# Two graph layers on one core: W1 moved behind the attention sum, softmax rows transposed through VectorE and DRAM

## The chip, the core and the metric

The kernel runs on one NeuronCore of a Trainium2 chip. The metric is the time of one launch in device microseconds, the median of several runs. The profile is that of one execution, whose span is counted from the first to the last instruction. The engines are TensorE (PE in the profile, its weight loads PEld), VectorE (DVE), ScalarE (ACT), GpSimd (POOL) and SyncE (SP, which only issues DMAs here). [...]

## What is computed

There are 16 batches of 1024 nodes with 512 features, one dense 1024 x 1024 matrix adj with about 6% nonzeros, and two layers. All is float32. The reference, cut to what matters:

```
# layer 0
h = relu(layernorm(x));  x = x + (adj @ h) @ weight + bias
# layer 1
h = relu(layernorm(x)) @ W
s1, s2 = h @ a1, h @ a2                       # a1, a2: the halves of a
e = leaky_relu(s1[:, :, None] + s2[:, None, :], 0.2) * adj
h_prime = softmax(e, axis=2) @ h
x = x + elu(h_prime + beta * h)
```

## The kernel before

The nodes of a batch are 8 chunks of 128 rows, two halves of 4 chunks. For each batch the kernel does this:

- norm0_part and norm0_end (lines 143 to 155) make hn, the normalised input of layer 0, with nodes on the partitions. GpSimd adds the bias to x in place (line 148).
- y_half (line 157) multiplies hn with the transposed adj (adjT, made once by transpose_adj on TensorE at the start): 4 x 8 products for a half of the nodes. The result yT has features on the partitions.
- out0 (line 173) multiplies yT with W0 for one chunk, adds x, and takes the statistics of the new x.
- h_transposes (line 191) makes u, the normalised input of layer 1 without its 1/std, transposes it on TensorE through an identity (group ut) and copies it to uT. h_products (line 201) multiplies uT with W1 to hw, and forms the row sums s1 and s2 against a1 and a2. diag (line 221) is s2 on the diagonal of a 128 x 128 tile.
- spread_s2 (line 230) multiplies ones with diag, which gives s2 of all nodes on each partition (group pb).
- softmax_row (line 242) makes one chunk of exp(e - max) and 1/sum. adj lies in SBUF all the time (adj_sb).
- row_transposes (line 260) transposes that chunk on TensorE in 8 pieces (group pt); ScalarE copies them to pT.
- attend (line 269) multiplies pT with hw, adds beta times hw, applies elu and adds x; the result is stored from SP.

The loop over batches (line 309) puts layer 0 of batch b+1 beside layer 1 of batch b. The order on each engine isn't only that of the source: the builder of the program orders the instructions of each engine when they have become ready, with the source's order as priority, and adds all waits. A tile of a pool waits for a free buffer among the pool's.

A float32 product of 128 x 128 with 128 x 512 is two MATMUL instructions in the profile; a transpose is one.

Of the kernel before, what the change touches and what calls it, by code (L numbers as in the profile page):

```python
"""Two pre-norm graph layers: x + (adj @ relu(LN(x))) W0 + bias, then x + elu(GAT(relu(LN(x)))).

All matrix products are float32 on the tensor engine.  The nodes (1024) are cut into 8 chunks of
128; chunk c of a batch holds nodes c*128 .. c*128+127 on the partitions.

Layer 0 of batch b+1 is interleaved with layer 1 of batch b, so that the tensor engine has matrix
products while the other engines work on norms and softmax rows.
"""
# [10 lines left out]
F32 = mybir.dt.float32  # L19
# [3 lines left out]
P = 128  # L23
ALPHA = 0.2
EPS = 1e-5
# [4 lines left out]
def kernel(  # L30
# [13 lines left out]
    NCH = N // P  # chunks of nodes  # L44
    DC = D // P  # chunks of features
    HC = NCH // 2  # chunks of nodes in a half
    HN = N // 2

    const = ctx.enter_context(tc.tile_pool(name="const", bufs=1))
    xpool = ctx.enter_context(tc.tile_pool(name="xpool", bufs=5))  # L50
    big = ctx.enter_context(tc.tile_pool(name="big", bufs=1))
    work = ctx.enter_context(tc.tile_pool(name="work", bufs=2))
    stat = ctx.enter_context(tc.tile_pool(name="stat", bufs=2))
    ps_y = ctx.enter_context(tc.tile_pool(name="ps_y", bufs=2, space=bass.MemoryType.PSUM))
    ps_t = ctx.enter_context(tc.tile_pool(name="ps_t", bufs=3, space=bass.MemoryType.PSUM))
    ps_m = ctx.enter_context(tc.tile_pool(name="ps_m", bufs=3, space=bass.MemoryType.PSUM))

# [1 line left out]
    ident = const.tile([P, P], F32, name="ident")  # L59
    make_identity(nc, ident)  # L60
    ones = const.tile([P, P], F32, name="ones")
    nc.gpsimd.memset(ones, 1.0)
    eps_c = const.tile([P, 1], F32, name="eps_c")
    nc.gpsimd.memset(eps_c, EPS)
# [3 lines left out]
    def load_x(b, h, engine):  # L68
        t = xpool.tile([P, HC, D], F32, tag="x", name=f"x_{b}_{h}")
        engine.dma_start(  # L70
            out=t, in_=x[b, h * HN : (h + 1) * HN, :].rearrange("(c p) d -> p c d", p=P)
        )
        x_tiles[b, h] = t

    def xc(b, c):
        return x_tiles[b, c // HC][:, c % HC, :]

    adj_sb = [const.tile([P, N], F32, name=f"adj_{c}") for c in range(NCH)]
    adjT = [const.tile([P, N], F32, name=f"adjT_{c}") for c in range(NCH)]
    load_x(0, 0, nc.scalar)  # L80
    for c in range(HC):
        nc.sync.dma_start(out=adj_sb[c], in_=adj[ts(c, P), :])
    load_x(0, 1, nc.scalar)
    w0_sb = const.tile([P, DC, D], F32, name="w0_sb")
    nc.scalar.dma_start(out=w0_sb, in_=w0.rearrange("(c p) o -> p c o", p=P))
    bias_bc = const.tile([P, D], F32, name="bias_bc")
    nc.scalar.dma_start(out=bias_bc, in_=bias.partition_broadcast(P))
    for c in range(HC, NCH):
        nc.sync.dma_start(out=adj_sb[c], in_=adj[ts(c, P), :])
    w1_sb = const.tile([P, DC, D], F32, name="w1_sb")  # L90
    nc.scalar.dma_start(out=w1_sb, in_=w1.rearrange("(c p) o -> p c o", p=P))
    a1_bc = const.tile([P, D], F32, name="a1_bc")
    nc.scalar.dma_start(out=a1_bc, in_=a[0:D, :].rearrange("f o -> (f o)").partition_broadcast(P))
    a2_bc = const.tile([P, D], F32, name="a2_bc")
    nc.scalar.dma_start(
        out=a2_bc, in_=a[D : 2 * D, :].rearrange("f o -> (f o)").partition_broadcast(P)
    )
    beta_c = const.tile([P, 1], F32, name="beta_c")
    nc.scalar.dma_start(out=beta_c, in_=beta.partition_broadcast(P))
# [7 lines left out]
    def transpose_adj(h):  # L107
        for mc in range(NCH):
            pt = ps_t.tile([P, HC, P], F32, tag="tr", name=f"adjt_{h}_{mc}")
            for k in range(HC):  # L110
                nc.tensor.transpose(pt[:, k, :], adj_sb[h * HC + k][:, ts(mc, P)], ident)
            copy(mc, adjT[mc][:, ts(h, HN)], pt.rearrange("p k n -> p (k n)"))

# [1 line left out]
    mvs = {}  # L115
    rstds = {}

    def stats(layer, b, c):
        if c == 0:
            mvs[layer, b] = stat.tile([P, NCH, 2], F32, tag=f"mv{layer}", name=f"mv{layer}_{b}")  # L120
        st = stat.tile([P, 6], F32, tag="bn", name=f"bn{layer}_{b}_{c}")
        nc.vector.bn_stats(st, xc(b, c))  # L122
        nc.vector.bn_aggr(mvs[layer, b][:, c, :], st)

    def inv_std(layer, b):
        mv = mvs[layer, b]
        sd = stat.tile([P, NCH], F32, tag=f"sd{layer}", name=f"sd{layer}_{b}")
        nc.scalar.activation(sd, mv[:, :, 1], AF.Sqrt, bias=eps_c)
        r = stat.tile([P, NCH], F32, tag=f"rstd{layer}", name=f"rstd{layer}_{b}")
        nc.vector.reciprocal(r, sd)  # L130
        rstds[layer, b] = r

    def centred_relu(dst, layer, b, c):
        """relu(x - mean): relu(LN(x)) without its positive factor 1/std."""
        nc.vector.tensor_scalar(  # L135
            dst, xc(b, c), mvs[layer, b][:, c, 0:1], 0.0, op0=ALU.subtract, op1=ALU.max
        )

# [1 line left out]
    hns = {}  # L140
    yTs = {}

    def norm0_part(b, c):
        stats(0, b, c)
        hn = big.tile([P, D], F32, tag=f"hn{c}", name=f"hn_{b}_{c}")
        centred_relu(hn, 0, b, c)
        hns[b, c] = hn
        nc.gpsimd.tensor_tensor(xc(b, c), xc(b, c), bias_bc, op=ALU.add)  # L148

    def norm0_end(b):  # L150
        inv_std(0, b)
        for c in range(NCH):
            nc.scalar.activation(
                hns[b, c], hns[b, c], AF.Copy, scale=rstds[0, b][:, c : c + 1]
            )

    def y_half(b, h):
        """yT[d, n] = sum_m hn[m, d] adj[n, m] for half of the nodes n."""
        yT = big.tile([P, DC, HN], F32, tag="yT", name=f"yT_{b}_{h}")
        for dc in range(DC):  # L160
            py = ps_y.tile([P, HN], F32, tag="py", name=f"py_{b}_{h}_{dc}")
            for mc in range(NCH):
                nc.tensor.matmul(  # L163
                    py,
                    hns[b, mc][:, ts(dc, P)],
                    adjT[mc][:, ts(h, HN)],
                    start=(mc == 0),
                    stop=(mc == NCH - 1),
                )
            copy(dc, yT[:, dc, :], py)  # L170
        yTs[b, h] = yT

    def out0(b, c):
        """x1 = x + bias + y W0, in place of x, and its statistics."""
        h, k = divmod(c, HC)
        po = ps_m.tile([P, D], F32, tag="pm", name=f"po_{b}_{c}")
        for dc in range(DC):
            nc.tensor.matmul(  # L178
                po, yTs[b, h][:, dc, ts(k, P)], w0_sb[:, dc, :],
                start=(dc == 0), stop=(dc == DC - 1),  # L180
            )
        nc.vector.tensor_tensor(xc(b, c), po, xc(b, c), op=ALU.add)  # L182
        stats(1, b, c)

# [1 line left out]
    hws = {}  # L186
    s1s = {}
    s2bcs = {}
    diags = {}

    def h_transposes(b, c):
        u = work.tile([P, D], F32, tag="u", name=f"u_{b}_{c}")
        centred_relu(u, 1, b, c)
        pt = ps_t.tile([P, DC, P], F32, tag="tr", name=f"ut_{b}_{c}")
        for dc in range(DC):
            nc.tensor.transpose(pt[:, dc, :], u[:, ts(dc, P)], ident)  # L196
        uT = work.tile([P, DC, P], F32, tag="uT", name=f"uT_{b}_{c}")
        copy(c, uT, pt)
        return uT

    def h_products(b, c, uT):
        """h = relu(LN(x1)) W1 with its row sums against a1 and a2."""
        ph = ps_m.tile([P, D], F32, tag="pm", name=f"ph_{b}_{c}")
        for dc in range(DC):
            nc.tensor.matmul(  # L205
                ph, uT[:, dc, :], w1_sb[:, dc, :], start=(dc == 0), stop=(dc == DC - 1)
            )
        hw = big.tile([P, D], F32, tag=f"hw{c}", name=f"hw_{b}_{c}")
        nc.scalar.activation(hw, ph, AF.Copy, scale=rstds[1, b][:, c : c + 1])  # L209
        hws[b, c] = hw  # L210
        if c == 0:
            s1s[b] = stat.tile([P, NCH], F32, tag="s1", name=f"s1_{b}")
            diags[b] = work.tile([P, NCH, P], F32, tag="e", name=f"diag_{b}")
        s2 = stat.tile([P, 1], F32, tag="s2", name=f"s2_{b}_{c}")
# [8 lines left out]
    def h_layer(b):  # L223
        uT = h_transposes(b, 0)
        for c in range(NCH):
            after = h_transposes(b, c + 1) if c + 1 < NCH else None
            h_products(b, c, uT)
            uT = after
# [152 lines left out]
```

## Time and profile before

| | |
|---|---|
| time, median of 3 runs | 2896.78 us (2895.94 to 2896.81) |
| span of the profiled execution | 2893.5 us |
| granted TensorE clock | 0.998 of full |
| read from and written to HBM | 40.63 MB, 33.55 MB |
| mean DMA traffic | 26 GB/s |
| ACT_TABLE_LOAD | 32, of 1.283 us |

A line of a group in the profile has the source line, engine and operation, then the tile written and those read, the shapes and the count; behind the first bar the time in total and the mean of one in ns; behind the second the idle time of the engine ahead of the group, and what ended it. A line of the timeline has the start in us, the duration, and in brackets the idle time ahead of it.

### The profile page before, as it was taken

The page shows a single profiled execution, that of the slowest core. Times are in us where ns is not written, and L with a number is a line of the kernel's source. Part 1 is how long each engine was busy: PE and PEld are TensorE (multiplying, and loading weights), DVE is VectorE, ACT ScalarE, POOL GpSimd, SP SyncE. Part 2 cuts the span into 40 slices and gives each one's busy share as a digit, 9 for nine tenths or more (in the row PEclk, how much of TensorE's full clock was granted, in tenths as well). Part 3 has the DMA queues.
Part 4 walks back from the last instruction along what each step waited for, and adds up shares of the span by engine and source line. Part 5 has one row for each costly group of instructions (what it writes and reads, how often), then busy time and mean ns, then how long its engine had stood idle before and what let it go on. Part 6 is the DMA issues. An engine that isn't in the chain of part 4 may idle for free.

```text
span 2893.5 us, 21399 instructions
## 1 busy us (share of the span) xinstructions
PE 2852.3 (99%) x7808; PEld 1344.7 (46%) x7808; DVE 1336.0 (46%) x2616; ACT 803.9 (28%) x1240; POOL 547.3 (19%) x520
## 2 busy tenths in 40 slices
PE   7999999999999999999999999999999999999988
PEld 3444444444444444444444444444444444444444
DVE  2364353643536344363543536435364353644444
ACT  1132232322323223232222323223232232322323
POOL 1112022130211203112031120312112022130213
PEclk9999999999999999999999999999999999999999
DMA  4001000000000000001010000000001000000000
GB/s 171 0 5 36 18 30 29 8 33 19 30 29 12 33 15 33 26 23 36 1 36 22 29 30 4 33 22 30 29 8 33 18 29 29 8 33 4 19 11 29
DMA packets 38216, 75.54 MB, mean 26 GB/s; under 512 B 2913, under 2 KB 2913, under 8 KB 38113
## 3 DMA queue, kind: packets, MB, share of 16 engines
q1 hardware_dynamic: 35424, 69.22, 7.0%
q10 hardware_dynamic: 2688, 4.98, 0.5%
q8 instruction: 61, 1.00, 0.1%
q14 instruction: 43, 0.34, 0.0%
HBM read 40.63 MB, written 33.55 MB: 26 GB/s over the span
## 4 chain that ended last, share of the span: by engine, by line
PE 93%; DVE 4%; ACT 2%; DMA 1%; issue 0%; POOLq 0%; POOL 0%; ACTq 0%; DVEq 0%
PE pa L275 30%; PE py L163 30%; PE ph L205 15%; PE po L178 12%; PE pt L265 4%; PE ut L196 2%; DVE e L246 1%; DVE e L248 1%; ACT e L255 1%; DVE x L182 1%; DMA bias_bc<-in_L_gnn_bias_dram 1%; ACT e L245 1%; DVE bn L122 0%; DVE s2bc L103 0%; DVE u L135 0%
## 5 line engine op out<-in xcount | busy, mean ns | idle before, releaser
L275 PE MATMUL pa<-hw,pT 128*128 128x512 f32 x2048 | 902.5, 592 | 0.0
L163 PE MATMUL py<-adjT,hn 128*128 128x512 f32 x2048 | 892.6, 593 | 0.0
L163 PEld LDWEIGHTS py<-adjT,hn 128*128 128x128 f32 x2048 | 386.9, 190 | 474.5 <-issue 461.1
L275 PEld LDWEIGHTS pa<-hw,pT 128*128 128x128 f32 x2048 | 380.6, 190 | 436.4 <-issue 429.4
L205 PE MATMUL ph<-w_sb,uT 128*128 128x512 f32 x1024 | 458.1, 592 | 0.2 <-ACT uT L105 0.2
L178 PE MATMUL po<-w_sb,yT 128*128 128x512 f32 x1024 | 449.8, 592 | 0.3 <-DVE yT L103 0.3
L280 POOL TENSOR_SCALAR t<-z 128x512 f32<-128x512 f32 x128 | 78.7, 615 | 1228.3 <-DVE z L279 1179.9
L178 PEld LDWEIGHTS po<-w_sb,yT 128*128 128x128 f32 x1024 | 194.4, 190 | 245.0 <-issue 243.9
L205 PEld LDWEIGHTS ph<-w_sb,uT 128*128 128x128 f32 x1024 | 187.0, 190 | 199.0 <-issue 194.9
L103 DVE COPY yT<-py 128x512 f32<-128x512 f32 x64 | 44.3, 692 | 477.7 <-PE py L163 477.7
L148 POOL TENSOR_TENSOR x<-x,bias_bc 128x512 f32<-128x512 f32 x128 | 166.5, 1314 | 416.9 <-DVE hn L135 315.6
L255 ACT ACTIVATE e<-e,nmx 128x1024 f32<-128x1024 f32 x128 | 147.2, 1150 | 321.8 <-DVE nmx L253 321.3
L246 DVE SCALAR_TENSOR_TENSOR e<-e 128x1024 f32<-128x1024 f32 x128 | 196.5, 1546 | 71.1 <-ACT e L245 68.2
L272 POOL TENSOR_SCALAR t<-hw,beta_c 128x512 f32<-128x512 f32 x128 | 139.1, 1086 | 469.6 <-ACT hw L209 460.5
L217 DVE CUSTOM_DVE_ANT_0 prod<-hw,a_bc 128x512 f32<-128x512 f32 x256 | 185.2, 723 | 89.3 <-ACT hw L209 86.0
L284 POOL TENSOR_TENSOR z<-z,x 128x512 f32<-128x512 f32 x128 | 162.2, 1267 | 227.8 <-DVE z L283 227.8
L266 ACT COPY pT<-pt 128x512 f32<-128x512 f32 x256 | 136.4, 584 | 221.6 <-PE pt L265 221.5
L209 ACT ACTIVATE hw<-ph,rstd 128x512 f32<-128x512 f32 x128 | 88.0, 687 | 390.7 <-PE ph L205 390.7
L283 DVE SCALAR_TENSOR_TENSOR z<-t,z 128x512 f32<-128x512 f32 x128 | 88.7, 693 | 217.2 <-ACT t L281 217.2
L279 DVE SCALAR_TENSOR_TENSOR z<-pa,rs,t 128x512 f32<-128x512 f32 x128 | 96.1, 751 | 178.9 <-PE pa L275 177.2
L122 DVE BATCH_NORM_STATS2 bn<-x 128x6 f32<-128x512 f32 x256 | 170.6, 684 | 16.3 <-DMA x<-in_x_dram 12.9
L248 DVE CUSTOM_DVE_ANT_0 e<-e,adj 128x1024 f32<-128x1024 f32 x128 | 173.9, 1360 | 2.3
(41 smaller groups left out, 1408.1 us busy)
## 6 DMA issues: line engine op xcount, KB each, us to landing
out_dram<-z SPq DMA_DIRECT2D x128, 256.0 KB, 2.0
x<-in_x_dram SPq DMA_DIRECT2D x30, 1024.0 KB, 6.0
adj<-in_adj_dram SPq DMA_DIRECT2D x8, 512.0 KB, 9.1
x<-in_x_dram ACTq DMA_DIRECT2D x2, 1024.0 KB, 12.6
w_sb<-in_L_gnn_weight_dram ACTq DMA_DIRECT2D x1, 1024.0 KB, 22.1
w_sb<-in_L_gnn_W_dram ACTq DMA_DIRECT2D x1, 1024.0 KB, 11.2
a_bc<-in_L_gnn_a_dram ACTq DMA_DIRECT2D x2, 256.0 KB, 5.7
bias_bc<-in_L_gnn_bias_dram ACTq DMA_DIRECT2D x1, 256.0 KB, 19.7
```

What stands on the lines that cost most here:

```text
L122: nc.vector.bn_stats(st, xc(b, c))
L148: nc.gpsimd.tensor_tensor(xc(b, c), xc(b, c), bias_bc, op=ALU.add)
L163: nc.tensor.matmul(py, hns[b, mc][:, ts(dc, P)], adjT[mc][:, ts(h, HN)], start=(mc == 0), stop=(mc == NCH - 1),)
L178: nc.tensor.matmul(po, yTs[b, h][:, dc, ts(k, P)], w0_sb[:, dc, :], start=(dc == 0), stop=(dc == DC - 1),)
L205: nc.tensor.matmul(ph, uT[:, dc, :], w1_sb[:, dc, :], start=(dc == 0), stop=(dc == DC - 1))
L217: nc.vector.tensor_tensor_reduce(out=prod, in0=hw, in1=a_bc, scale=1.0, scalar=0.0, op0=ALU.mult, op1=ALU.add, accum_out=s,)
L246: nc.vector.scalar_tensor_tensor(e, e, ALPHA, e, op0=ALU.mult, op1=ALU.max)
L248: nc.vector.tensor_tensor_reduce(out=e, in0=e, in1=adj_sb[c], scale=1.0, scalar=LOWEST, op0=ALU.mult, op1=ALU.max, accum_out=mx,)
L255: nc.scalar.activation(e, e, AF.Exp, bias=nmx, accum_out=sm)
L272: nc.gpsimd.tensor_scalar(t, hws[b, c], beta_c, 1.0, op0=ALU.mult, op1=ALU.mult)
L275: nc.tensor.matmul(pa, pT[:, jc, :], hws[b, jc], start=(jc == 0), stop=(jc == NCH - 1))
L284: nc.gpsimd.tensor_tensor(z, z, xc(b, c), op=ALU.add)
```

## The change

Layer 1 is regrouped. Since the attention sum is linear, softmax(e) @ (u W1) is (softmax(e) @ u) W1. So:

- u (with its 1/std) stays with nodes on the partitions and is the stationary operand of attend; the product with W1 comes behind, in out1. No u is transposed.
- s1 and s2 are dot products of u with W1 a1 and W1 a2 (v1_bc, v2_bc, made once through DRAM). spread_s2 writes s2 to DRAM and reads it back to all partitions.
- beta h is added by beta times the row's sum on the diagonal of the unnormalised softmax row.
- The softmax row is transposed in 32 x 32 blocks on VectorE. Four DMAs (one for each group of 32 partitions) write the blocks to DRAM and one reads them back into pT. A half of pT is one tile, and attend works on a half, as y_half does.
- adj isn't kept in SBUF; each softmax row loads its chunk again (two buffers, tag "adj").
- The leaky relu is one Prelu on ScalarE. 1/std is a power on GpSimd, for two chunks at a time. elu is formed from Relu and Exp.
- x is loaded twice, once for the norm (load_x, 4 buffers) and once with the bias as residual (load_res, 10 buffers). The tile zT shares a pool of 3 buffers with yT.

The core of the diff, the new lines:

```diff
+    def load_x(b, c):
+        t = xs.tile([P, D], F32, tag="x", name=f"x_{b}_{c}")
+        nc.sync.dma_start(out=t, in_=x[b, ts(c, P), :])
...
+    def load_res(b, c):
+        t = x1p.tile([P, D], F32, tag="x1", name=f"x1_{b}_{c}")
+        nc.sync.dma_start(out=t, in_=x[b, ts(c, P), :])
+        nc.gpsimd.tensor_tensor(t, t, bias_bc, op=ALU.add)
...
+    def inv_std(r, nb, mv):
+        k = r.shape[1]
+        nc.gpsimd.tensor_scalar(r, mv[:, :, 1], EPS, 1.0, op0=ALU.add, op1=ALU.mult)
+        nc.gpsimd.tensor_tensor(r, r, half[:, 0:k], op=ALU.pow)
+        nc.vector.scalar_tensor_tensor(nb, mv[:, :, 0], -1.0, r, op0=ALU.mult, op1=ALU.mult)
...
+    def out0(b, g):
...
+        inv_std(r, nb, mv)
+        for k in range(2):
+            c = 2 * g + k
+            u = nat.tile([P, D], F32, tag=f"u{c}", name=f"u_{b}_{c}")
+            nc.scalar.activation(
+                u, x1s[b, c], AF.Relu, scale=r[:, k : k + 1], bias=nb[:, k : k + 1]
+            )
+            us[b, c] = u
+            for v, s in ((v2_bc, s2s[b]), (v1_bc, s1s[b])):
...
+                nc.vector.tensor_tensor_reduce(
+                    out=prod, in0=u, in1=v, scale=1.0, scalar=0.0,
+                    op0=ALU.mult, op1=ALU.add, accum_out=s[:, c : c + 1],
+                )
...
+    def spread_s2(b):
+        d = dram.tile([N], F32, tag="s2d", name=f"s2d_{b}")
+        nc.sync.dma_start(out=d.rearrange("(c p) -> p c", p=P), in_=s2s[b])
+        t = work.tile([P, N], F32, tag="s2bc", name=f"s2bc_{b}", bufs=1)
+        nc.sync.dma_start(out=t, in_=d[:].partition_broadcast(P))
...
+    def softmax_row(b, c):
...
+        w = work.tile([P, N], F32, tag="adj", name=f"adj_{b}_{c}")
+        nc.sync.dma_start(out=w, in_=adj[ts(c, P), :])
+        e = work.tile([P, N], F32, tag="e", name=f"e_{b}_{c}", bufs=3)
+        nc.scalar.activation(e, s2bcs[b], AF.Prelu, bias=s1s[b][:, c : c + 1], alpha=ALPHA)
...
+        nc.vector.tensor_tensor_reduce(
+            out=w, in0=e, in1=w, scale=1.0, scalar=LOWEST,
+            op0=ALU.mult, op1=ALU.max, accum_out=mx,
+        )
...
+        nc.scalar.activation(w, w, AF.Exp, bias=nmx, accum_out=sm)
...
+        nc.vector.scalar_tensor_tensor(
+            w[:, ts(c, P)], ident, bs, w[:, ts(c, P)], op0=ALU.mult, op1=ALU.add
+        )
+        t = work.tile([P, G, NCH, Q], F32, tag="e", name=f"t_{b}_{c}", bufs=3)
+        nc.vector.transpose(
+            t.rearrange("p g j r -> p j g r"), w.rearrange("p (j g r) -> p j g r", g=G, r=Q)
+        )
+        d = dram.tile([G, Q, G, NCH * Q], F32, tag="pd", name=f"pd_{b}_{c}", bufs=4)
+        for s in range(G):
+            nc.sync.dma_start(
+                out=d[:, :, s, :].rearrange("g q n -> q g n"),
+                in_=t[ts(s, Q)].rearrange("q g j r -> q g (j r)"),
+            )
+        nc.sync.dma_start(
+            out=pTs[b, h][:, i].rearrange("p s j r -> p (s j r)"),
+            in_=d.rearrange("g q s n -> (g q) (s n)"),
+        )
...
+    def attend(b, h):
+        zT = fT.tile([P, DC, HN], F32, tag="fT", name=f"zT_{b}_{h}")
+        pT = pTs[b, h].rearrange("p i s j r -> p j (i s) r")
+        for dc in range(DC):
+            pz = ps_a.tile([P, HN], F32, tag="pa", name=f"pz_{b}_{h}_{dc}")
+            for jc in range(NCH):
+                nc.tensor.matmul(
+                    pz, us[b, jc][:, ts(dc, P)], pT[:, jc],
+                    start=(jc == 0), stop=(jc == NCH - 1),
+                )
+            copy(dc, zT[:, dc, :], pz)
...
+    def out1(b, c):
...
+        nc.scalar.activation(r, po, AF.Relu, scale=rs[:, i, 0:1])
+        nc.scalar.activation(t, po, AF.Relu, scale=rs[:, i, 1:2])
+        nc.scalar.activation(t, t, AF.Exp, scale=-1.0)
+        nc.vector.scalar_tensor_tensor(t, t, -1.0, x1s[b, c], op0=ALU.add, op1=ALU.add)
+        nc.gpsimd.tensor_tensor(r, r, t, op=ALU.add)
+        nc.sync.dma_start(out=out[b, ts(c, P), :], in_=r)
...
+    for g in range(HC):
+        norm0(0, g)
+        transpose_adj(g)
...
     for b in range(B):
         more = b + 1 < B
...
+        spread_s2(b)
         if more:
             y_half(b + 1, 0)
...
+        for c in range(HC):
+            softmax_row(b, c)
         if more:
+            y_half(b + 1, 1)
+        for c in range(HC, NCH):
+            softmax_row(b, c)
+        for h in range(2):
+            attend(b, h)
+            for i in range(HC):
+                out1(b, h * HC + i)
+                if more:
+                    load_res(b + 1, h * HC + i)
+            if b + 2 < B:
+                for g in range(2):
+                    norm0(b + 2, 2 * h + g)
         if more:
+            for g in range(HC):
+                out0(b + 1, g)
```

The tags "u0" to "u7" have one buffer each, so u of batch b+1 is written when attend of batch b has read it.

## The prediction

> **What bounds the kernel now.** I read the page first (busy times, then the chain that ended last), then the groups by form, then the timelines of the middle and of both ends.
>
> ```profile
> PE 2852.3 (99%) x7808; PEld 1344.7 (46%) x7808; DVE 1336.0 (46%) x2616; ACT 803.9 (28%) x1240; POOL 547.3 (19%) x520
> ...
> PE 93%; DVE 4%; ACT 2%; DMA 1%; issue 0%; POOLq 0%; POOL 0%; ACTq 0%; DVEq 0%
> ```
>
> TensorE is busy all the time and is 93% of the chain. Every other engine has over half of the span free. So only TensorE's work, and new waits of TensorE, count.
>
> ```profile
> L265 PE MATMUL pt<-ident,e 128*128 128x128 f32 x1024 | 136.0, 277 | 10.1 <-ACT e L255 8.0
> L196 PE MATMUL ut<-ident,u 128*128 128x128 f32 x512 | 74.2, 273 | 0.0
> L235 PE MATMUL pb<-diag,ones 128*128 128x512 f32 x64 | 30.3, 593 | 1.7 <-DVE diag L221 1.7
> ```
>
> These three groups go. Their times overlap their neighbours', so the price comes from starts in the timeline of TensorE:
>
> ```profile
> 1097.63 1.04 PE L265 MATMUL pt<-ident,e 128*128 128x128 f32 x8
> 1098.50 7.03 PE L275 MATMUL pa<-hw,pT 128*128 128x512 f32 x16
> 1105.37 1.04 PE L265 MATMUL pt<-ident,e 128*128 128x128 f32 x8
> 1106.24 7.03 PE L275 MATMUL pa<-hw,pT 128*128 128x512 f32 x16
> ```
>
> Sixteen matmul instructions take 1105.37 - 1098.50 = 6.87 us, 0.4294 each; eight transposes 0.87 us, 0.1088 each. (A float32 product is two instructions.)
>
> Next, whether an engine keeps to the order of the source. It does not:
>
> ```profile
> 1067.33 0.69 DVE L182 TENSOR_TENSOR x<-po,x 128x512 f32<-128x512 f32 x1 [1.08 <-PE po L178]
> ...
> 1069.00 0.49 DVE L135 TENSOR_SCALAR u<-x,mv 128x512 f32<-128x512 f32 x1
> ```
>
> That u is the first of h_layer of the next batch, which the source calls some 140 us later. VectorE runs it as soon as its row is there. TensorE likewise fills waits with later y products (two py at 1079.15), and the SP queue issues x loads of later batches at 13 us. The builder orders each engine by readiness. But a queue, once ordered, stands behind its head: the waits of SP are 2795.2 us behind the output stores of L285.
>
> The ends:
>
> ```profile
> 25.29 1.28 ACT L128 ACT_TABLE_LOAD   x1 [25.29 <-DMA bias_bc<-in_L_gnn_bias_dram]
> ...
> 33.78 24.20 PE L163 MATMUL py<-adjT,hn 128*128 128x512 f32 x56
> ...
> 2822.04 3.68 PE L265 MATMUL pt<-ident,e 128*128 128x128 f32 x16 [8.05 <-ACT e L255]
> ```
>
> Dense y work starts at 33.8 us (30.3 counting the eight y instructions already done). The last batch waits 8.05 us for its first softmax row and 1.7 us for diag.
>
> [...]
>
> **Part by part.**
>
> TensorE. Gone: 1024 pt x 0.1088 = 111.4, 512 ut x 0.1088 = 55.7, 64 pb x 0.4294 = 27.5; together 194.6 us. Kept: y, out0 and the new attend and out1 are 4096 + 2048 instructions of the same 128x512 form, 6144 x 0.4294 = 2638, as before. The moving operand now has runs of 32 elements; I take the same rate (bounds 0 to +2% of attend's 880, 18 us). Per batch 177.1 becomes 164.9; the trace's period from 1004.40 to 1181.80 is 177.4, so the arithmetic holds.
>
> Other engines per batch, by the nearest rows. VectorE: norms 8 x 0.86, out0 8 x (0.69 + 0.86 + 2 x 0.80 + 0.15), rows 8 x 3.9 (product 1.44, diagonal 0.28, transpose estimated 1.5 between 1.2 and 2.4, four small 0.15), copies 5.5, end 5.5: about 75 us. ScalarE: Relus 11, rows 8 x 2.5, copies 4.7, end 15.6: 51; if Prelu needs its own table, two loads a row add 20. GpSimd: adds 20.6, 16 small inv_std operations of 0.1 to 1 us: 22 to 37. All far below 164.9: nothing on the path. Sqrt's table loads go, hidden before as well.
>
> DMA. A row reads 0.5 MB of adj, writes 0.5 MB in four pieces and reads it back, six issues on SP. With x twice, the output and s2 it is 19 MB a batch, 117 GB/s; the first 34 us of the trace carry 12.3 MB, with stretches near 400. Issues: 74 a batch x 0.37 us = 27 us of SP. Hidden, as throughput. The residual is loaded again when out1 frees a buffer of x1 (10 of them), and GpSimd adds bias behind out1's sums; the last chunk has some 20 us until its out0: nothing. The latency of the rows is what matters.
>
> The new wait. After the last out0 of a batch, TensorE has only the next batch's y (128 x 0.4294 = 55 us) before attend half 0, which needs rows 0 to 3 in pT. The chain: add and statistics 1.9 (1070.56 to 1072.44), inv_std 1.5 (0.6 to 4), Relu and dot products 3.6 (3 to 6): 7. s2 store, 4-byte pieces, 3 (2 to 6); broadcast load 512 KB 4 (3.3, between 256 KB and 1 MB, to 5.7, the landing of a_bc): s2 at 14 (10 to 22). Row 0: Prelu 1.15, product 1.44, exp 1.34, smalls and diagonal 0.6, transpose 1.5, six hand-overs of 0.2: 7.2; write 4 (3 to 6), read-back 3.5: 14.7. Row 0 lands at 29 (23 to 40). Row period p, the largest of: VectorE 3.9; DMA 1.5 MB, 4 to 5.5; two adj buffers, each held from issue (0.4, load 3.3) through the row's 7.2, (3.7 + 7.2) / 2 = 5.5; SP, where the read-back stands waiting for its four writes with the next row's writes, adj loads and x loads behind it: 1.6 + 0.4 + 0.4 + about 3.5 = 6. I take 6 (5 to 8). Row 3 lands at 29 + 18 = 47 (38 to 64) against 55: no stall at my value, up to 9 us a batch at the bound. Rows 4 to 7 have 41 us more (attend 27.5, out1 13.7) for 24. For small hand-overs (zT to out1, the third fT slot) I put 10 us in all (0 to 140 with the bounds above).
>
> The last batch has no y: the whole 47 (38 to 64) is idle instead of 9.8, +37, and 2 for a cold clock. After the last product: 7.9 us before, the same after.
>
> The start. y needs hn and half of adj only, and no longer ScalarE's wait for bias_bc; x comes in 256 KB pieces through four buffers, adj through two on ScalarE's queue[...]. I take y at 20 instead of 30.3: -10 (-16 to +5). v through DRAM hides beside y.
>
> Sum on the profiled span: 2893.5 - 194.6 + 39 - 10 + 10 = 2738. The runs' median stands 3.3 us above that span: 2741.
>
> **Rivals.**
> (1) Rows partly exposed: pieces and 4-byte stores near my bounds, row 3 at 57 to 64, a stall of 2 to 9 us in 15 batches: 2775 to 2885. For it: nothing in the trace shows the small transfers; against: 8 us of slack.
> (2) The SP queue serialises the rows, and the kernel is slower. If adj of row c+1 is issued only behind the read-back of row c, nothing is prefetched and p = 3.7 + 7.2 + 4 = 15, or less with a good order. Row 3 comes at 29 + 3p, row 7 at 29 + 7p against 96. The excess of the larger one is paid 15 times and the last batch pays more. The gain of 157 left after the ends is gone at about 10 us a batch: 29 + 7p = 106, p = 11. At p = 15 row 7 comes at 134, 38 us late: the last batch loses 27 before attend half 0 and 19 before half 1: 2741 + 15 x 38 + 46 = 3357. For it: SP does stand behind its head, and issues of adj in the first 10 us waited 6.5 us for an unrelated x load. Against: readiness orders SP too, and the adj load of row c+2 is ready when row c's writes are, ahead of the read-back.
> (3) It does not do what it says, TensorE's time hardly falls, because 32-element runs slow attend by 20% or more: 880 x 0.2 = 176, 2741 + 176 = 2917, about no change. Against: each run is 128 contiguous bytes.
>
> **How the numbers follow.** Forecast (no stall, 2705 to 2775) 0.62; rival 1 0.20; rival 2 0.12; rival 3 0.03; better ends, under 2705, 0.03. About 0.2% is what a measurement of this kernel can tell from no change. Faster 0.85, same 0.03, slower 0.12. The range 2700 to 2880 leaves out rival 2, most of rival 3 and the edges.
>
> **What would show it.** Right: no pt, ut, pb in the groups; periods near 165 us; TensorE waiting once for pT, 35 to 65 us near the end. Rival 1: a wait of pz for pT of a few us in each batch. Rival 2: waits above 10 us, SP waiting on writes to DRAM, rows over 11 us apart. Rival 3: attend's starts farther apart than 0.43. A SP queue ordered badly would make me most wrong.

## The result and the profile after

The changed kernel takes 2919.42 us (median of 4 runs, 2916.03 to 2924.95) against 2896.8 us before: ratio 1.0079, 95% interval 1.0065 to 1.0093. It is slower by 0.8%. The forecast was 2741 us.

First the page of the changed kernel: busy times, the chain that ended last, then groups.

```profile
PE 2699.1 (92%) x6208; PEld 1191.0 (41%) x6208; DVE 1060.9 (36%) x2608; ACT 800.1 (27%) x1185; POOL 450.3 (15%) x519
...
PE 49%; DMA 17%; DVE 16%; issue 7%; ACT 4%; POOL 4%; SPq 2%; DVEq 0%; POOLq 0%; ACTq 0%
...
L247 PE MATMUL pz<-pT,u 128*128 128x512 f32 x2048 | 920.7, 612 | 178.9 <-DMA pT<-pd 117.0
...
L205 ACT ACTIVATE e<-s2bc,s 128x1024 f32<-128x1024 f32 x128 | 145.4, 1136 | 250.8 <-DMA s2bc<-s2d 250.8
```

The work did go: pt, ut and pb are gone, and TensorE is busy 153.2 us less (2852.3 to 2699.1). But its idle time (span less busy) grew from 41.2 to 224.1 us, by 182.9. TensorE now holds 49% of the chain instead of 93%; DMA and VectorE have the rest. Most of the idle time stands ahead of one group, pz, the attention products: 178.9 us. ScalarE's first operation of a row (e) has waited 250.8 us in all for s2bc, the spread s2. (The releaser named there, and in the lines below, is that of the last event; it varies from batch to batch.)

One batch on TensorE, from the timeline of the changed kernel:

```profile
1427.22 30.08 PE L247 MATMUL pz<-pT,u 128*128 128x512 f32 x64 [8.42 <-DVE rs L236]
...
1471.77 27.70 PE L247 MATMUL pz<-pT,u 128*128 128x512 f32 x64 [0.74 <-issue]
...
1540.51 55.10 PE L134 MATMUL py<-adjT,hn 128*128 128x512 f32 x128
1603.74 16.83 PE L247 MATMUL pz<-pT,u 128*128 128x512 f32 x32 [8.13 <-DMA x<-in_x_dram]
```

(The last line goes up to 1620 us, where the stretch ends; whole, it is 64 products in 30.57 us.) Attend half 0 waits 8 us in each of these batches (105.8 us over batches 1 to 14; batch 0's waits for nothing), and then takes 30.08 us instead of 27.6. TensorE's clock has been lowered in the wait: the granted clock in the trace is 1.00 from 1363 to 1418 us, 0.71 in the mean from 1418 to 1427, 0.50 from 1427 to 1432 and 1.00 again from 1432 to 1440. Over the whole execution it is 0.966, against 0.998 before. Half 1 loses 0.74 us. Behind waits of 7 to 8 us 2.4 us are lost in the mean; s2_rows and s2_hop below show a loss of 1.5 to 1.8 us behind some waits of 2.0 to 3.2 us too. Half 1, with the same operand in runs of 32 elements, takes 27.70, so the operand isn't slow.

What the wait is for is read from the SP queue in the same stretch. y begins, and so the last out0 ends, at 1540.51:

```profile
1550.66 0.38 SPq L188 DMA_DIRECT2D s2d<-s  x1
1559.22 0.32 SPq L190 DMA_DIRECT2D s2bc<-s2d  x1
1570.75 5.28 SPq L226 DMA_DIRECT2D pd<-t  x6
1576.20 0.34 SPq L230 DMA_DIRECT2D pT<-pd  x1
...
1577.55 0.93 SPq L203 DMA_DIRECT2D adj<-in_adj_dram  x2
...
1587.44 5.34 SPq L226 DMA_DIRECT2D pd<-t  x6
...
1597.94 0.33 SPq L230 DMA_DIRECT2D pT<-pd  x1
```

Each line counts issues; a single one takes 0.32 to 0.38 us in these lines, and a duration well above that for each issue has time in it in which the queue stood. The 4 KB store of s2 is issued at 1550.66, and the broadcast load that needs it only at 1559.22, 8.6 us later. The adj loads of rows 2 and 3 leave at 1577.55, behind all eight writes of rows 0 and 1, so rows come in pairs 16.7 us apart (1570.75 to 1587.44). The read-back of row 3 leaves at 1597.94, and the product that needs it starts at 1603.74, 63.2 us after the last out0, against 55 us of y.

From VectorE's and then ScalarE's timeline in the same stretch, the last dot product for s2, the transpose of row 0, row 2's wait for its adj, and the first use of s2bc:

```profile
1549.93 0.69 DVE L177 CUSTOM_DVE_ANT_0 prod<-u,v_bc 128x512 f32<-128x512 f32 x1
...
1569.47 1.25 DVE L221 STREAM_TRANSPOSE t<-adj 128x1024 f32<-128x1024 f32 x1
...
1582.80 1.23 DVE L207 CUSTOM_DVE_ANT_0 adj<-e,adj 128x1024 f32<-128x1024 f32 x1 [7.01 <-DMA adj<-in_adj_dram]
```

```profile
1564.45 1.15 ACT L205 ACTIVATE e<-s2bc,s 128x1024 f32<-128x1024 f32 x1 [16.24 <-DMA s2bc<-s2d]
```

One thing stands in none of these lines. While the store of s2 is under way (1551 to 1559 us) the core's DMA engines are busy for 6% of the time and move 1 GB/s: the store is a delay and not a load. In the wait of attend (1595.6 to 1603.7) they are busy for 96% and move 361 GB/s, while two adj loads (at 1594.29) and four loads of x (at 1598.32) are issued around row 3's read-back. What this crowding adds to that read-back no run separates.

The list of transfers of the changed kernel (KB each, median us from issue to landing) has the price of the store:

```profile
s2bc<-s2d SPq DMA_DIRECT2D x16, 512.0 KB, 5.0
...
s2d<-s SPq DMA_DIRECT2D x16, 4.0 KB, 8.9
```

4 KB in 1024 pieces of 4 bytes take longer to land (8.9 us) than 512 KB (5.0 us).

The ends, from TensorE's timeline of the changed kernel: y of batch 0, y of batch 1 and the last attend.

```profile
31.65 29.86 PE L134 MATMUL py<-adjT,hn 128*128 128x512 f32 x64
...
129.37 6.46 PE L134 MATMUL py<-adjT,hn 128*128 128x512 f32 x8 [8.55 <-ACT hn L119]
...
2831.95 29.16 PE L247 MATMUL pz<-pT,u 128*128 128x512 f32 x64 [59.62 <-DMA pT<-pd]
```

y of batch 0 starts at 31.65 us (30.3 before), y of batch 1 has to wait for its hn, and the last attend waits 59.62 us, since no y of a next batch is there to hide the chain.

### The profile page after: what moved, and what is told of

Read it like the earlier page. It is cut to its first block, busy times and chain, and to the rows that moved or that the text cites. A ratio compares the mean times of both kernels' runs of the same rounds, so it can differ in the third digit from the quotient of the medians.

```text
span 2923.2 us, 19770 instructions
## 1 busy us (share of the span) xinstructions
PE 2699.1 (92%) x6208; PEld 1191.0 (41%) x6208; DVE 1060.9 (36%) x2608; ACT 800.1 (27%) x1185; POOL 450.3 (15%) x519
## 4 chain that ended last, share of the span: by engine, by line
PE 49%; DMA 17%; DVE 16%; issue 7%; ACT 4%; POOL 4%; SPq 2%; DVEq 0%; POOLq 0%; ACTq 0%
PE pz L247 30%; PE pq L259 11%; PE py L134 5%; DVE prod L177 5%; DMA s2d<-s 5%; PE po L159 3%; DMA adj<-in_adj_dram 3%; DMA pd<-t 3%; DMA pT<-pd 2%; DVE bn L102 2%; DMA s2bc<-s2d 2%; DVE x L163 2%; DVE adj L207 2%; POOL r L97 2%; DVE t L221 2%
## 5 line engine op out<-in xcount | busy, mean ns | idle before, releaser
L247 PE MATMUL pz<-pT,u 128*128 128x512 f32 x2048 | 920.7, 612 | 178.9 <-DMA pT<-pd 117.0
L134 PE MATMUL py<-adjT,hn 128*128 128x512 f32 x2048 | 890.6, 597 | 13.7 <-ACT hn L119 11.4
L247 PEld LDWEIGHTS pz<-pT,u 128*128 128x128 f32 x2048 | 400.5, 197 | 698.8 <-issue 520.6
L259 PE MATMUL pq<-w_sb,zT 128*128 128x512 f32 x1024 | 444.7, 593 | 0.0
L271 POOL TENSOR_TENSOR r<-r,t 128x512 f32<-128x512 f32 x128 | 161.9, 1265 | 1089.9 <-DVE t L270 1089.9
L259 PEld LDWEIGHTS pq<-w_sb,zT 128*128 128x128 f32 x1024 | 195.0, 190 | 244.5 <-issue 244.5
L207 DVE CUSTOM_DVE_ANT_0 adj<-e,adj 128x1024 f32<-128x1024 f32 x128 | 154.4, 1206 | 385.9 <-ACT e L205 221.4
L214 ACT ACTIVATE adj<-adj,nmx 128x1024 f32<-128x1024 f32 x128 | 147.0, 1148 | 525.9 <-DVE nmx L212 525.9
L205 ACT ACTIVATE e<-s2bc,s 128x1024 f32<-128x1024 f32 x128 | 145.4, 1136 | 250.8 <-DMA s2bc<-s2d 250.8
L177 DVE CUSTOM_DVE_ANT_0 prod<-u,v_bc 128x512 f32<-128x512 f32 x256 | 175.1, 684 | 45.0 <-ACT u L171 44.1
L221 DVE STREAM_TRANSPOSE t<-adj 128x1024 f32<-128x1024 f32 x128 | 158.9, 1241 | 0.2 <-DVE rs L236 0.2
## 6 DMA issues: line engine op xcount, KB each, us to landing
x<-in_x_dram SPq DMA_DIRECT2D x256, 256.0 KB, 4.5
out_dram<-r SPq DMA_DIRECT2D x128, 256.0 KB, 2.1
```

What stands on the lines that cost most here:

```text
L134: nc.tensor.matmul(py, hns[b, mc][:, ts(dc, P)], adjT[mc][:, ts(h, HN)], start=(mc == 0), stop=(mc == NCH - 1),)
L177: nc.vector.tensor_tensor_reduce(out=prod, in0=u, in1=v, scale=1.0, scalar=0.0, op0=ALU.mult, op1=ALU.add, accum_out=s[:, c : c + 1],)
L205: nc.scalar.activation(e, s2bcs[b], AF.Prelu, bias=s1s[b][:, c : c + 1], alpha=ALPHA)
L207: nc.vector.tensor_tensor_reduce(out=w, in0=e, in1=w, scale=1.0, scalar=LOWEST, op0=ALU.mult, op1=ALU.max, accum_out=mx,)
L214: nc.scalar.activation(w, w, AF.Exp, bias=nmx, accum_out=sm)
L221: nc.vector.transpose(t.rearrange("p g j r -> p j g r"), w.rearrange("p (j g r) -> p j g r", g=G, r=Q))
```

## The experiments

My theory A: the chain from the last out0 of a batch to row 3 in pT sets the time; the 4-byte store, the adj loads behind the writes, and the first norms are links of it. Rivals: the rows are paced by something else (copies in VectorE's order, throughput of the transfers), so that one link repaired shifts the wait and saves nothing. All times are compared with runs of the kernel before on the same chip (2896.6 to 2897.8 us).

The table has all runs. "First attend" is the start of batch 0's attend half 0 on TensorE; "period" is the mean distance of those starts from batch 0 to 14; the waits are TensorE's idle time ahead of attend half 0 and half 1, in total over batches 0 to 14 (half 0) and all 16 (half 1); "last gap" is the wait of batch 15's attend half 0. In s2_rows and s2_pb another 8.27 and 9.46 us of wait of batch 15 stand ahead of TensorE's own s2 product. All in us, from the timelines.

| kernel | first attend | period | wait half 0 | wait half 1 | last gap | time | ratio to before (95%) |
|---|---|---|---|---|---|---|---|
| changed kernel | 192.28 | 176.13 | 105.8 | 13.6 | 59.62 | 2919.42 | 1.0065 to 1.0093 |
| s2_rows | 189.46 | 172.68 | 16.2 | 14.7 | 44.01 | 2856.7 | 0.9847 to 0.9882 |
| s2_pb | 190.58 | 175.64 | 0 | 35.8 | 37.88 | 2903.58 | 1.0015 to 1.0031 |
| adj_act | 197.07 | 174.37 | 87.4 | 0 | 60.70 | 2912.42 | 1.0035 to 1.0065 |
| norm_first | 186.93 | 176.44 | 113.0 | 11.4 | 60.16 | 2928.22 | 1.0094 to 1.0127 |
| s2_dve | 188.79 | 167.50 | 16.9 | 13.1 | 53.87 | 2793.46 | 0.9627 to 0.9656 |
| s2_dve_adj | 187.32 | 164.80 | 0 | 0 | 53.61 | 2751.8 | 0.9481 to 0.9512 |
| s2_dve_adj_out | 187.33 | 164.80 | 0 | 0 | 52.19 | 2754.32 | 0.9491 to 0.9519 |
| all4 | 177.07 | 164.85 | 1.5 | 0 | 52.06 | 2742.93 | 0.9451 to 0.9479 |
| s2_hop | 190.46 | 166.88 | 22.7 | 0 | 55.48 | 2785.83 | 0.9604 to 0.9632 |
| start | 180.75 | 165.03 | 3.8 | 0 | 51.51 | 2748.85 | 0.9476 to 0.9504 |
| best3 | 181.68 | 164.87 | 2.3 | 0 | 50.81 | 2744.62 | 0.9464 to 0.9490 |
| pt_pe | | | | | | 2891.97 | 0.9974 to 0.9987 |

All columns but the last two come from one profiled execution of each kernel. For the changed kernel this is the slowest of its four (2924.95 us), for adj_act the fastest of its four (2904.47), so these two rows differ by more than the medians do.

**One link alone, in four runs.** s2_rows: TensorE transposes s2 (128 x 8), and the store has eight rows of 512 bytes.

```diff
-        nc.sync.dma_start(out=d.rearrange("(c p) -> p c", p=P), in_=s2s[b])
+        pt = ps_t.tile([P, HC, P], F32, tag="tr", name=f"s2t_{b}")
+        nc.tensor.transpose(pt[:NCH, 0, :], s2s[b], ident)
+        s2r = stat.tile([NCH, P], F32, tag="s2r", name=f"s2r_{b}")
+        nc.vector.tensor_copy(s2r, pt[:NCH, 0, :])
+        nc.sync.dma_start(out=d.rearrange("(c p) -> c p", p=P), in_=s2r)
```

> s2 is transposed once per batch on TensorE (one 128x8 instruction) and stored as 8 rows of 512 bytes in place of 1024 single floats; all else as in the changed kernel. Theory A (the chain from out0 to row 3 ends 7.7 us too late in each batch, and the 4-byte store is 8.5 us of it): the store lands in 2 to 3.5 us, the hand-over adds 1, so row 3 comes 4.5 to 6 us earlier, the wait of attend half 0 falls from 7.7 to 2 to 3 us, the wait before the last batch from 59.6 to about 54, and the time to 2919 - 15 x 5 - 5 = about 2840; less if the clock no longer drops. Theory B (the rows behind s2 are held by their own period, or attend's first half is slow by its strided operand): the wait or the slow half stays, the time within 15 us of 2919.

Measured 2856.7 us, 63 less than the changed kernel, and 17 more than expected. The store and the load that needs it, from the SP queue of this kernel, then a batch on TensorE:

```profile
1524.95 0.30 SPq L192 DMA_DIRECT2D s2d<-s2r  x1
1526.18 0.33 SPq L194 DMA_DIRECT2D s2bc<-s2d  x1
```

```profile
1351.76 0.37 PE L189 MATMUL s2t<-ident,s 128*8 128x128 f32 x1 [3.15 <-DVE s L177]
1351.93 49.60 PE L134 MATMUL py<-adjT,hn 128*128 128x512 f32 x112
1402.72 27.70 PE L251 MATMUL pz<-pT,u 128*128 128x512 f32 x64 [1.19 <-DVE yT L88]
```

The same 4 KB take 1.2 us from store to load instead of 8.6, and attend's wait falls from 8 us to 1.2. But TensorE works in order: the tiny s2t stands between y products and waits 3.15 us for VectorE's dot products. The 112 y instructions behind it take 49.60 us where 112 x 0.4294 = 48.1. So some 4.7 us of the repair are lost again. Rows 0 to 3 also come farther apart, 8.8 us instead of 7.2 in the mean of 16 batches: part of what an earlier s2 gives is lost in the rows behind it, as theory B had it.

s2_pb: s2 spread as in the kernel before, by ones times diag on TensorE, with no store and no load.

```diff
+            nc.vector.tensor_scalar(diags[b][:, c, :], ident, s2s[b][:, c : c + 1], None, op0=ALU.mult)
...
-        nc.sync.dma_start(out=t, in_=d[:].partition_broadcast(P))
+            nc.tensor.matmul(
+                pb, ones, diags[b][:, ts(h, HC), :].rearrange("p c n -> p (c n)"),
+                start=True, stop=True,
+            )
+            copy(h, t[:, ts(h, HN)], pb)
```

> spread_s2 as in the kernel before: ones times diag(s2) on TensorE, copied from PSUM, in place of the store to DRAM and the broadcast load; all else as in the changed kernel. Theory A: the chain loses the store (8.5) and the load (5.2) and gets about 2.5 us, so row 3 comes 11 us earlier, the wait of attend half 0 is gone and with it the cold clock; the product costs TensorE 1.7 us in 16 batches. Time 2919 - 14 x 11.5 + 27 - 11 = about 2775, faster than the kernel before. The wait before the last batch falls from 59.6 to about 49. Theory B (row period or strided operand): attend half 0 still starts late or still takes 29 to 30 us, time 2919 + 27 = 2946.

Measured 2903.58 us: far from the 2775 expected. Attend half 0 waits for nothing now, but the same happens as in s2_rows, and half 1 waits:

```profile
1368.51 1.14 PE L195 MATMUL pb<-diag,ones 128*128 128x512 f32 x2 [3.54 <-DVE diag L185]
...
1463.36 27.70 PE L256 MATMUL pz<-pT,u 128*128 128x512 f32 x64 [2.76 <-issue]
```

The SP queue shows why half 1 waits in this batch: row 7's read-back (L239) stands behind two output stores (L281), at which the queue stands for some 3 us, and a residual load.

```profile
1454.35 3.79 SPq L281 DMA_DIRECT2D out_dram<-r  x2
...
1458.78 0.33 SPq L239 DMA_DIRECT2D pT<-pd  x1
```

So 7.1 us of wait a batch (mean of 15) give way to about 3.6 us ahead of pb, 2.2 ahead of half 1 (mean of 16), 1.7 of pb's own products (4 x 0.4294) and slowed products behind the waits: here 112 y instructions in 49.93 us.

adj_act: the softmax rows' adj loads on ScalarE's queue.

```diff
-        nc.sync.dma_start(out=w, in_=adj[ts(c, P), :])
+        nc.scalar.dma_start(out=w, in_=adj[ts(c, P), :])
```

> The loads of adj for the softmax rows go on ScalarE's queue in place of SP's, where they stand behind the writes of the next row; all else as in the changed kernel. Theory A, its second part (row 2 waits 7 us for its adj because the load is issued behind row 1's writes and row 0's read-back): the load of row 2 is issued some 6 us earlier, the row pair period falls from 16.8 us to about 12, row 3 comes 4 to 6 us earlier: time 2919 - 15 x 5 to 8 = 2800 to 2845. Theory B (two buffers or the DMA engines limit the rows, or ScalarE's queue now stands where SP's stood): period stays near 16.8, time within 20 us of 2919 or above.

Measured 2912.42 us, far from theory A's 2800 to 2845 and inside theory B's range. The first four rows are hardly faster: their read-backs in one batch leave at 1393.04, 1399.46, 1407.87 and 1414.44, 7.1 us apart (7.0 in the mean of 16 batches, 7.2 in the changed kernel). Over all eight rows of a batch the mean distance falls from 9.5 to 6.6 us, and half 1's waits are gone, with the output stores still on SP. But half 0 still waits for row 3 behind the slow store, 87.4 us in total. A faster pace of the later rows alone doesn't do it.

norm_first: in the prologue the norms of batch 1 are called ahead of batch 0's out0 (two loops exchanged).

> In the prologue the norm of batch 1 stands before out0 of batch 0 in the source, in place of behind it; all else as in the changed kernel. Theory C (y of batch 1 waits 8.6 us and then runs in pieces until 140.7 us because VectorE takes the statistics of batch 1 only behind all of out0): y of batch 1 runs without a wait from about 121 us, its end moves from 192.3 to about 176; but then batch 0's attend meets the late rows too and waits some 8 us plus 3 for the clock. Time 2919 - 16 + 11 = 2905 to 2915. If the x loads are what holds it: no change.

Measured 2928.22 us, 13 above the expected range. y of batch 1 now runs from 122.36, but batch 0's first attend waits 7.99 us for its rows, so it starts only 5.35 us sooner, and this is lost again later: 113.0 us of waits of half 0. That the median is 8.8 us above the changed kernel's isn't explained: the two profiled executions took the same (2924.36 and 2924.95).

**The store repaired without TensorE.** s2 lies in a tile of 32 columns, VectorE turns it in 32 x 32 blocks, and four DMAs store 8 pieces of 128 bytes each.

```diff
-            s2s[b] = stat.tile([P, NCH], F32, tag="s2", name=f"s2_{b}")
+            s2s[b] = stat.tile([P, Q], F32, tag="s2", name=f"s2_{b}")
+            nc.gpsimd.memset(s2s[b], 0.0)
...
-        nc.sync.dma_start(out=d.rearrange("(c p) -> p c", p=P), in_=s2s[b])
+        nc.vector.transpose(s2r, s2s[b])
+        for g in range(G):
+            nc.sync.dma_start(
+                out=d.rearrange("(c g q) -> g c q", g=G, q=Q)[g],
+                in_=s2r[g * Q : g * Q + NCH, :],
+            )
```

> s2 is laid out in rows by one 32x32-block transpose on VectorE (128x32, about 0.2 us) instead of by TensorE, and stored by four transfers of 8 pieces of 128 bytes; the rest is the changed kernel. Theory A (the chain from the last out0 to row 3 sets the wait of attend half 0, and the 4-byte store is 7 us of it): the store takes about 2.5 us with its four issues, s2 comes some 6 us sooner, the wait of 7.7 us falls to under 2, its cold clock (some 2.6 us) goes too, and unlike the version with TensorE's own s2 product no 3 us wait stands ahead of it: period about 168 to 170, time 2815 to 2845. Theory B (the wait comes from the rows' own pace, s2 being early only lets them queue): the rows' pair period grows as in the version with s2t, attend half 0 still waits 3 us or more, time 2860 to 2890.

Measured 2793.46 us: theory A, and better than its range. From the SP queue and from TensorE of this kernel:

```profile
1652.95 1.31 SPq L192 DMA_DIRECT2D s2d<-s2r  x4
1655.24 0.34 SPq L197 DMA_DIRECT2D s2bc<-s2d  x1
```

```profile
1531.08 27.70 PE L254 MATMUL pz<-pT,u 128*128 128x512 f32 x64 [1.94 <-DVE mx L214]
```

8.6 us became 2.3; the waits of half 0 fell from 105.8 to 16.9 us in all, and behind waits this short attend takes 27.70 us. The edit of the store, with the layout of s2 that it needs and nothing else, takes 126 us off the time.

**The other links on top.** s2_dve_adj has s2_dve's edit and adj_act's.

> As s2_dve, and the softmax rows' adj loads on ScalarE's queue instead of SP's. Theory A: the rows come 6.7 us apart instead of 8.3 as in the run with that edit alone, so row 3 is ahead of the last y product and attend half 0 waits for nothing but its yT copies; period 166 to 168, time 2795 to 2830. Theory B (rows are paced by yT copies and other work in VectorE's order): no gain over s2_dve beyond 5 us.

Measured 2751.8 us, below the expected range. Attend waits in no batch but the last; in the timeline of TensorE attend follows on y without a bracket, and 164.81 us later again:

```profile
1505.71 27.63 PE L254 MATMUL pz<-pT,u 128*128 128x512 f32 x64
...
1615.58 55.10 PE L134 MATMUL py<-adjT,hn 128*128 128x512 f32 x128
1670.52 27.63 PE L254 MATMUL pz<-pT,u 128*128 128x512 f32 x64
```

VectorE's wait for adj (at the product of e and adj) is 2.3 us in total, against 152.2 us in s2_dve. adj_act alone had saved 7 us (20 between the two profiled executions); here the same edit saves 42. With s2 early it does bring rows 0 to 3 closer together, from 7.7 to 6.9 us apart in the mean; while the store was late it was only one of two links in a row.

s2_dve_adj_out: the output stores are issued by GpSimd as well.

> As s2_dve_adj, and the output stores issued by GpSimd behind its own sum instead of by SP, so that SP carries only x loads and the rows' writes and read-backs. Theory A: row 7's read-back no longer stands behind an output store, half 1 waits for nothing; 5 to 15 us less than s2_dve_adj (0.3 to 1 us a batch), the last batch's gap some us shorter. Theory B (SP's order is no longer what is late): within 5 us of s2_dve_adj.

Measured 2754.32 us: theory B. With adj off SP, the order of what is left on it is no longer what is late.

all4: that, and norm_first's edit.

> As s2_dve_adj_out, and batch 1's norms ahead of batch 0's out0 in the prologue. That edit alone brought batch 0's attend 5 us sooner and a wait of 8 us gave it back. Theory A (the gain was lost to the waits of the rows, which are now gone): 4 to 8 us less than s2_dve_adj_out. Theory B (out0 of batch 0 is on the path to its rows, and norms ahead of it delay them): no gain or a loss up to 5 us.

Measured 2742.93 us, ratio 0.9465 (0.9451 to 0.9479). The first attend is 10.3 us sooner (187.33 to 177.07), and this time it isn't given back: the time falls by 11, more than the 4 to 8 expected. The gain of norm_first had been lost to the rows' waits.

best3: all4 with the output stores on SP again.

> s2 by VectorE, adj on ScalarE's queue and batch 1's norms ahead of batch 0's out0, but the output stores left on SP's queue. Theory A (with s2 early and adj off SP, SP's order no longer sets anything, and moving the output stores cost 2.5 us in the run before): 2738 to 2744. Theory B (norms first gains only together with the stores on GpSimd's queue): 2748 to 2755.

Measured 2744.62 us, 0.6 above what theory A gave; all4 and best3 can't be told apart. These two are the fastest kernels of the study.

**Is it the delay?** s2_hop: s2_dve_adj, with s2 read back from DRAM into 8 partitions and stored once more ahead of its broadcast. It puts a delay into the chain, with two more issues on SP's queue and 8 KB of traffic.

> The version with s2 by VectorE and adj on ScalarE's queue (2751.8 us), and one more pass of s2 through SBUF and DRAM ahead of its broadcast load: a delay of the chain by about 4 us (a load and a store of 4 KB in 512-byte rows), and next to no load on any engine. In that version row 3's read-back lands 1 us ahead of the product that needs it. Theory A (the chain from out0 to row 3 alone sets the wait, and its slack is used up): 3 to 4 us of wait a batch and 0.5 to 2 us of slowed clock, 15 times, and 4 in the last batch: 2805 to 2840. Theory B (the changed kernel's time came from the 4-byte store's load on queues and memory, not from its delay): no more than 10 us above 2751.8.

Measured 2785.83 us, 34 us more than without the hop and 19 below the expected range. From its SP queue:

```profile
1649.09 0.26 SPq L197 DMA_DIRECT2D s2q<-s2d  x1
...
1651.66 0.35 SPq L201 DMA_DIRECT2D s2bc<-s2e  x1
```

The hop costs 1651.66 - 1649.09 = 2.6 us, not 4, and the period grows by 166.88 - 164.80 = 2.1 us. So a delay alone, of 2.6 us, comes back at 0.8 us a batch for each us. Theory B (load on queues and memory) had at most 10 us in all; theory A had counted 4 us for the hop.

**One part of the change alone.** pt_pe: W1 behind the sum and s2_dve_adj's edits, but the softmax rows transposed on TensorE as before, without DRAM.

```diff
+        for k in range(2):
+            pt = ps_t.tile([P, HC, P], F32, tag="tr", name=f"pt_{b}_{c}_{k}")
+            for q in range(HC):
+                nc.tensor.transpose(pt[:, q, :], w[:, ts(k * HC + q, P)], ident)
+            copy(k, pTs[b, h][:, ts(k, HC), ts(i, P)], pt)
```

> One part of the change alone: W1 behind the attention sum and no u transposes, with s2 by VectorE and adj on ScalarE's queue, but the softmax rows transposed on TensorE as in the kernel before, with no write to DRAM and no read-back. Theory A (each part of the change frees TensorE of what the prediction counted, and the arrangement in DRAM costs only latency): TensorE takes 1024 x 0.1088 = 111 us more than in the version at 2751.8, the last batch's gap shrinks by the write and read-back of a row and by the faster row pace, 15 to 35 us, so 2825 to 2855, still below the kernel before by 40 to 70. Theory B (DRAM writes and read-backs slow the other transfers and cost the same): within 20 us of 2751.8.

Measured 2891.97 us, 140 above s2_dve_adj and outside the range of both theories. The line of its transposes among the groups by form:

```profile
L230 PE MATMUL pt<-ident,adj 128*128 128x128 f32 x1024 | 149.7, 283 | 56.1 <-DVE rs L234 32.9 <-ACT adj L221 13.0 <-ACT pT L90 10.1
```

out0 of the last batch starts at 2732.33 and that of eight batches before at 1333.44, a period of 174.9 us: 10.1 more than 164.8, where the transposes' own 64 x 0.1088 = 7.0 were expected. TensorE waits 56.1 us ahead of them, 27 in the last batch and some 1.9 in each other. Some 1.1 us a batch I can't place. Against the 177.4 of the kernel before the period is only 2.5 us shorter, where the missing ut and pb should give (55.7 + 27.5) / 16 = 5.2. So in this form (adj loaded again for each row, s2 through DRAM) W1 behind the sum saves next to nothing by itself, 5.5 us in all; the gain is in the rows that leave TensorE.

**The start.** start: all4, with the first adj loads on GpSimd's queue, each adj transpose called ahead of the norms beside it, and batch 0's residual loads behind y's first half.

> The version at 2742.9 us, with the first adj loads on GpSimd's queue instead of ScalarE's (where they stand behind Relus and copies), each adj transpose called ahead of the norms beside it, and the residual loads of batch 0 behind y's first half. Theory A (the start was late because of the order on ScalarE's, VectorE's and SP's queues): y starts at 20 to 25 us instead of 31.5 and the time falls by 6 to 12 us, 2731 to 2737. Theory B (the start is bound by the transfers themselves or by x's four buffers): y within 3 us of 31.5, time within 4 us of 2742.9.

Measured 2748.85 us: y starts at 33.62 us, later than all4's 31.54. This miss leaves the start unexplained in part. In its trace VectorE takes products of W1 with a ahead of part of batch 0's statistics and waits 8.07 us for a_bc, so the run changed more than the one thing it was meant to.

## Why the prediction was wrong

The step that failed is "Row 3 lands at 29 + 18 = 47 (38 to 64) against 55: no stall at my value", and with it "10 us in all" for hand-overs. Measured in the batch shown, row 3 is used at 63.2 us behind the last out0, 8 us after y has ended. The chain was the right one; its terms were too small. Here they are, with the predicted ones behind them:

- Dot products done, store issued: 10.2 us (7). VectorE takes statistics of a later batch in between (four of 0.69 us and their aggregates).
- Store of s2: 8.6 us (3, bounds 2 to 6). Outside its own bounds, and the largest single miss. My 3 us was an estimate next to the 2.0 us in which a 256 KB store landed in the kernel before (`out_dram<-z SPq DMA_DIRECT2D x128, 256.0 KB, 2.0`); no row showed pieces of 4 bytes, and I kept too close to the nearest one.
- Broadcast load: 5.2 us (4). s2 comes at 23.9 us (14, bounds 10 to 22).
- Row 0: 6.3 us to the end of its transpose (7.2, in which the transpose's 1.5 was an estimate of mine that no row showed; it takes 1.25); write and read-back issued 5.5 us later (4).
- Read-backs of rows 0 to 3: (1597.94 - 1576.20) / 3 = 7.25 us a row (6, bounds 5 to 8). The reason given, SP standing with the next adj loads behind it, was right in the changed kernel's order: the adj loads of rows 2 and 3 leave behind eight writes, and row 2 waits 7.01 us for its adj.
- Row 3's read-back, from issue to use: 5.8 us (3.5), with the DMA engines 96% busy.

The misses add up to some 16 us, twice the slack of 8; the store alone is 5.6 of them. So the mechanism was on the page, as rival 1, with 63 inside its 57 to 64, and I gave it 0.20. Its price was too low as well, 2775 to 2885, which would still have been faster than before: it had no term for TensorE's clock behind a wait, and none for the start.

Where the time is can be counted on the traces, changed kernel against all4, whose span of 2741.1 us lies 3 us above the sum that the prediction made (2738). The difference is 182.1 us:

- First attend: 192.28 - 177.07 = 15.2.
- Fourteen periods: 14 x (176.13 - 164.85) = 157.9. Of the 11.3 us of a period, 7.6 are the wait of half 0 (105.8 over 14), 0.9 that of half 1, 2.2 the slowed products of half 0 (27.63 us in batch 0, 30.04 in the mean behind a wait); 0.6 is left over.
- From batch 14's attend to batch 15's: 11.8, mostly the last gap (59.62 against 52.06) and the slowed half 0 of batch 14.
- End: -2.8.

Point by point:

- TensorE's saving of 194.6 us was right: without waits the period is 164.80 us in s2_dve_adj, predicted 164.9. In the changed kernel the 12.6 us saved of each batch's 177.4 met 11.3 us of waits and slow clock.
- "Other engines: nothing on the path" was right for busy time and wrong for order: VectorE's statistics stand in the chain.
- "Hidden, as throughput" was right for the mean (109 GB/s over the changed kernel's span; s2_dve_adj moves the same 319 MB without the waits), but the transfers come in bursts: in the wait of attend the DMA engines are busy for 96% of the time.
- The last batch: 47 predicted, 59.62 measured, 52 with the store repaired.
- The start was "y at 20 instead of 30.3". It is at 31.65, and y of batch 1, which I left out, waits 8.55, 0.46 and 2.43 us for its hn. The experiments repaired the second (all4) and not the first.
- Prelu: one table load in the whole trace (1.28 us), so the 20 us a batch that I held possible aren't there. Rival 3 fell with half 1's 27.70 us. Of rival 2's marks, SP does wait for writes (117.7 us in all ahead of the read-backs) and rows 1 and 2 are 11.8 us apart, but the rows' mean is 7.25 and no wait of a middle batch is above 10 us; it is not the queue alone but store, queue and VectorE's order together.
- all4's agreement with 2738 is in part chance: its y starts 11.5 us later and its last gap is 5 us longer than predicted, while the 10 us for hand-overs fell away.

That the store's delay is the main cause is shown: s2_dve changes it alone for 126 us, and s2_hop puts a delay back. The place of the adj loads in SP's queue is worth another 42 us, shown by s2_dve_adj behind the repaired store. VectorE's order in the chain is read from the trace, and no run changes it. Not settled are the start's first 31 us, the effect of DMA engines that are busy for 96% on the last read-back, and 1 us a batch in pt_pe.

## What to carry to other kernels

When work leaves the engine that bounds a kernel, write down the whole latency chain that takes its place, against the time that hides it, and don't let the slack hang on a link whose price no row shows: here 8 us of slack rested on a store that took 5.6 us more than assumed. Values that lie one to a partition and must go through DRAM were best laid out in rows first here (2793 against 2919 us), and not on the engine that bounds the kernel (2857), where even a tiny product waited 3.15 us in order. The links in a row didn't add here: adj_act saved 7 us alone (20 in the profiled executions) and 42 us behind the other repair, so a repair that shows nothing alone isn't refuted.

## What the runs showed of the hardware

- 4 KB stored in 1024 pieces of 4 bytes land in 8.9 us (median of 16), 2 KB of v in 512 pieces in 9.9 us. From store to dependent load the same 4 KB take 1.2 us as eight rows of 512 bytes, and 2.3 us as 32 pieces of 128 bytes in four DMAs.
- TensorE's products behind a wait of 7 to 8 us take 2.4 us longer (30.04 against 27.63 for 64, the mean behind 14 waits of which one was of 4.9 us), behind one of 3.15 us in s2_rows still 1.5 us, behind most of 1 to 2 us next to nothing (27.70). The length of the wait alone doesn't decide here: in s2_hop waits of 2.04 and 2.27 us cost 1.8 and 1.7 us (29.40 and 29.28), one of 2.38 us next to nothing (27.70), and in s2_pb half 1 behind one of 2.27 us took 29.40 us, behind one of 3.02 us 27.70.
- In the kernel before TensorE was slow behind its wait of 8.05 us too: the sixteen transposes take 3.47 us from start to start (16 x 0.1088 = 1.7 in the middle of the trace), at a granted clock of 0.50 from 2822 to 2826 us against 1.00 from 2800 to 2813. The prediction's 2 us for a cold clock in the last batch agree with that.
- In s2_dve, where the adj loads stand behind the rows' writes on SP's queue, VectorE waits 152.2 us for adj; in s2_dve_adj, with them on ScalarE's, it waits 2.3 us, with the bytes the same (319.4 MB).
- VectorE's transpose of 128 x 1024 float32 in 32 x 32 blocks takes 1.24 us, that of 128 x 32 0.21 us.
